# A bucket table in two parts: its first part filled uncleared from the first group on, and one register load for four row windows

## The chip, the cores and the metric

The kernel runs on one core of a Trainium2 chip. The metric is the device time of one execution in microseconds, as the median of several runs; less is better.

## The reference

Two graph layers over 6250 nodes with 128 features and 100000 edges, which are sorted by `dst`, while `src` is random:

```python
h = silu(concat([x[src], x[dst], radial(edge_weight)]) @ Wm1 + bm1)
m = silu(h @ Wm2 + bm2) @ Wm3 + bm3
out = segment_sum(m, dst)
u = silu(concat([x, out]) @ Wu1 + bu1) @ Wu2 + bu2
x = layernorm(x + silu(u @ Wi1 + bi1) @ Wi2 + bi2)

xt = logmap0(x)
att = sigmoid(concat([xt[src], xt[dst], edge_attr]) @ att_w.T + att_b)
s = xt + segment_sum(xt[src] * att, src) \
       + segment_sum(edge_attr, src) / max(count_src, 1) \
       + segment_sum(edge_attr, dst) / max(count_dst, 1)
x = layernorm(x + proj(expmap0(s)))
```

The sums over `dst` are easy, since the edges come in that order. The sums over `src` need the 100000 rows of `edge_attr` moved into an order by `src`, and this is what the change is about.

## The kernel before

**Stages.** The edges go in 98 groups (`NG`) of 1024, each as eight blocks `b` of 128 rows (one row per partition). An opening stage writes the projected node features `p_src` and `p_dst` to DRAM. The edge loop runs over the groups. The node rounds run over the 49 blocks of 128 nodes, four at a time, so 13 rounds. The attention stage runs over the groups again. A final stage sums the last rows and writes the output.

**Bucket tables.** A block of 128 nodes is a bucket, and there are 49 (`NB`). A row of `edge_attr`, with a one, the attention weight and the node's number within its bucket beside it (`RW` = 132 values), is sent to its `src` bucket by an indirect DMA on POOL (`scatter`, L814), 128 rows at a time. Blocks 0 to 2 of every group go to the table `early` (`first_t`, 896 rows for each bucket, `FIRST`). Blocks 3 to 7 go to four tables `late`, one for each stretch of groups (`GENS`: from group 0, 31, 62 and 83). The attention stage reads the tables back bucket by bucket (`bucket_load`, L1567), and TensorE sums the rows with one-hot matrices.

**Slots.** `place(g)` gives each row of group g its slot: TensorE counts how many rows went to the same bucket before (`rank`), and VectorE adds the bucket's beginning (`first`) and writes the row numbers to `to_i` (L1139). Rows that find no slot go to dump rows at the table's end (`dumps`). A group's first scatter needs `to_i` of that group.

**Clears.** Every bucket surely gets 640 of the 896 rows of `early`; the rest may stay empty and is set to zero first (`fills`, `clear`): nine DMAs for `early` (of the last bucket all rows, of the 48 others rows 640 to 895, 32 rows of each at a time), and 29 for `late`. They are issued on SP in the edge loop, two in each of the first five groups and then one in every second group (L1277). The scatters to `early` wait for the clears of `early`.

**The order of the edge loop** is written by hand. In group g, for each half, SP issues the loads `lw` of the `p_dst` rows of group g+2 (`load_rows`: four windows, for each a register load of its first row and a DMA), `near` of group g+2, `attr` of group g+1, and a clear; POOL issues four gathers (`ga`, L1080) of group g+2 and then at most one scatter to `early` of group g; TensorE, ScalarE and VectorE do the two layers of group g, and VectorE does `prepare` and `place` of group g+1:

```python
if clear and (g < LAG - 1 or i % 4 == 0):
    nc.sync.dma_start(*clear.pop(0))
gather(g + 2, range(4 * half, 4 * half + 4))
if g < NG and early(g, half) is not None:
    scatter(g, early(g, half), attrs[g][0][:, early(g, half)])
```

`early(g, half)` names the block that the loop scatters. Of the three early blocks of a group two are scattered in the loop. The third, and in every fifth group one more (`left`), is left to the middle. Of groups 0 to 5 (`LAG` = 6) all three are left to the middle.

**The middle** is a list of units of up to three such blocks (`middle`, `move_middle`, L1321 to L1340): SP loads the rows again, ScalarE copies the column of node numbers (L1335, L1338), POOL scatters them. Three units stand in each node round before TensorE's work; what is left comes after the last round. SP and POOL follow the written order here, the other engines a scheduler's. Units use four tiles in turn, so that a load waits for the scatter four units before.

**The attention stage** needs, for the logits of its first group, the statistics of all nodes: after the last round come `rstd` (L1455), norms and logarithms (L1468 to L1494), and their split into three bfloat16 parts. ScalarE then writes the attention weights into the rows of blocks 3 to 7 (L1666, L1669), and POOL scatters them to `late`.

Of the kernel before, what the change touches and what calls it, by code (L numbers as in the profile page):

```python
# [16 lines left out]
P = 128  # L17
# [9 lines left out]
ET = mybir.EngineType  # L27
# [504 lines left out]
W = 64  # L532
WE = 256

RW = 132


EARLY = ((1, 2), (0, 2), (0, 1))
LATE = (3, 4, 5, 6, 7)


LAG = 6

# [15 lines left out]
FIRST = (896, 640)  # L559
GENS = ((0, 512, 304), (31, 512, 304), (62, 384, 192), (83, 256, 116))  # L560
# [42 lines left out]
def window_path(ctx, tc, bad, x, src, dst, edge_attr, edge_weight, Wm1, bm1, Wm2, bm2, Wm3, bm3,  # L603
                Wu1, bu1, Wu2, bu2, Wi1, bi1, Wi2, bi2, att_w, att_b, out):
    nc = tc.nc
    ordered = ExitStack()
    ordered.enter_context(tc.manual_schedule())
    N, F = x.shape
# [17 lines left out]
    def windows(g):  # L626
        return min(4, NWIN - 4 * g)
# [5 lines left out]

    first_t = dram.tile([NB * FIRST[0] + 6 * P, RW], F32, name="early")
    lates = [dram.tile([NB * cap + 10 * P, RW], F32, name=f"late{j}") for j, (_, cap, _) in enumerate(GENS)]

    early_of = dram_disjoint_views(first_t[:, :], 6)
    lates_of = [dram_disjoint_views(t[:, :], 10) for t in lates]

    def stretch(g):  # L640
        return sum(g >= lo for lo, _, _ in GENS) - 1

    def table_of(g, b):

        return early_of[b + g % 2 * 3] if b < 3 else lates_of[stretch(g)][b - 3 + g % 2 * 5]

# [12 lines left out]
    dumps = const.tile([P, len(GENS), 2, 8], F32, name="dumps")  # L659
    nc.vector.memset(caps[:, :, :3], float(FIRST[0]))  # L660
    for j, (_, cap, _) in enumerate(GENS):
        nc.vector.memset(caps[:, j, 3:], float(cap))
        for b0, n, c in ((0, 3, FIRST[0]), (3, 5, cap)):
            nc.gpsimd.iota(dumps[:, j, :, b0:b0 + n], pattern=[[n * P, 2], [P, n]], base=NB * c,
                           channel_multiplier=1, allow_small_or_imprecise_dtypes=True)
# [52 lines left out]
    NL = 12  # L718
# [58 lines left out]
    first = sent.tile([P, 8, NG], F32, name="first")  # L777
    base_i = keep.tile([1, 4, NG], I32, name="base_i")
    badc = keep.tile([P, 1], F32, name="badc")
# [90 lines left out]
    with tc.tile_pool(name="init", bufs=1) as init, \  # L870
# [70 lines left out]
        def spread():  # L941
            pbase = initp.tile([P, 4, P], F32, name="pi")
            for k in range(4):
                nc.tensor.matmul(pbase[:, k, :NG], lhsT=basex[:, k], rhs=ident[:NG, :NG],
                                 start=True, stop=True)
            nc.vector.tensor_copy(base_i, pbase[:1, :, :NG])
            nc.vector.tensor_copy(baseb, pbase[:, :, :NG])
# [20 lines left out]
        def begins():  # L968

            for b0, b1, lo, hi_, cap in [(0, 3, 0, NG, FIRST[0])] + [  # L970
                    (3, 8, GENS[j][0], GENS[j + 1][0] if j + 1 < len(GENS) else NG, GENS[j][1])
                    for j in range(len(GENS))]:
                nc.vector.tensor_scalar(first[:, b0:b1, lo:hi_], hif[:, 0, b0:b1, lo:hi_], float(cap),
                                        None, op0=OP.mult)
# [77 lines left out]
    with tc.tile_pool(name="ework", bufs=2, reuse_waits="tile") as ework, \  # L1052
# [13 lines left out]

        def load_rows(g):
            for k in range(windows(g)):
                at = nc.values_load(base_i[0:1, k, g:g + 1], engines=(ET.SP,), min_val=0,
                                    max_val=ROWS - W, skip_runtime_bounds_check_because="clamped")  # L1070
                nc.sync.dma_start(lws[(4 * g + k) % NL][:W], p_dst[bass.ds(at, W)])

# [49 lines left out]
        def place(g):  # L1122
# [11 lines left out]

            over = ework.tile([P, 8], F32, name="over")
            nc.vector.tensor_tensor(over, slot, caps[:, j], op=OP.is_ge)
            nc.vector.tensor_add(slot, slot, first[:, :, g])
            nc.vector.scalar_tensor_tensor(slot, over, 1e6, slot, op0=OP.mult, op1=OP.add)
            nc.vector.tensor_tensor(to_i[:, :, g], slot, dumps[:, j, g % 2], op=OP.min)  # L1139

            for q, (end, cap, lo) in enumerate((
# [80 lines left out]
        def add_up(i):  # L1222
            g, k0, kk = part_of(i)
            if kk <= 0:
                return
            ps = sums.pop(i)
            for k in range(kk):
                at = nc.values_load(base_i[0:1, k0 + k, g:g + 1], engines=(ET.DVE,), min_val=0,
                                    max_val=ROWS - W, skip_runtime_bounds_check_because="clamped")
# [34 lines left out]
        prepare(0, 1)  # L1264
        place(0)
        for g in range(NG + 2):
            for half in range(2):
# [100 lines left out]
    with tc.tile_pool(name="nwork", bufs=2, reuse_waits="tile") as nwork, \  # L1368
# [5 lines left out]
        base_f = nwork.tile([P, NW], F32, name="bits", bufs=1)[:1]  # L1374
        nc.vector.tensor_copy(base_f, base_i.rearrange("o k g -> o (k g)"))
        pw_ = npp.tile([F, 4, P], F32, name="pu")
# [174 lines left out]
    with tc.tile_pool(name="bwork", bufs=2, reuse_waits="tile") as bwork, \  # L1551
# [4 lines left out]
        def bucket_load(us):  # L1556

            nonlocal n_load
            at = n_load % 4 * BR * RW
            n_load += 1  # L1560
            bts = []
            for i, h0, nh in us:
                t, cap = AT[i]
                c = cap // P
                bt = acc[:, 2, at:at + nh * c * RW].rearrange("p (h c f) -> p h c f", h=nh, f=RW)
                at += nh * c * RW
                nc.sync.dma_start(  # L1567
                    bt.rearrange("p h c f -> p h (c f)"),
                    t[h0 * cap:(h0 + nh) * cap].rearrange("(h p c) f -> p h (c f)", p=P, c=c))
                bts.append(bt)  # L1570
            return bts
# [278 lines left out]
```

## Time and profile before

| | |
|---|---|
| median of three runs | 2189.34 us (2189.02 to 2191.48) |
| the profiled execution: its time | 2187.51 us |
| the profiled execution: its span | 2185.6 us |
| mean granted TensorE clock | 0.85 |
| indirect DMAs on POOL | 782 gathers, 782 scatters |
| DMA moved | 412.75 MB, mean 189 GB/s |

The edge loop's gathers begin at 43.7 us of the span and its last scatter starts at 1275.6; the middle's scatters go from 1281.5 to 1446.3, the attention stage's from 1449.7 to 2090.6; the rest is the final stage. An indirect DMA's bar on POOL is the time that the engine spends on issuing it; the transfer itself lands later. "issue" as a releaser means that the engine waited for nothing that the profile shows. In a line of the timeline the first number is the start, the second the duration, and the bracket at the end holds the idle time before the instruction and what ended it. A wait for several semaphores is put down to the one that came last by the profile.

### The profile page before, as it was taken

To read this page: it belongs to the slowest core of one execution; us is meant where nothing else is said; L and a number is where in the kernel's file an instruction comes from. 1 tells how busy PE (TensorE), PEld (TensorE's weight loads), DVE (VectorE), ACT (ScalarE), POOL (GpSimd) and SP (SyncE) were. 2 spreads that over 40 slices of the span, in tenths; PEclk is the share of its full clock that TensorE was granted. 3 is DMA by queue.
4 is the path that set the end of the run, shared out by engine and by line. 5 is a ranking of instruction groups with operands and counts; after the bars stand their busy time and mean duration, and the time that the engine had idled before them with its cause. 6 is when DMAs were issued, how large, how long until landed. Compare 5 with 4: busy or idle time off the path is not lost. (4 is left out here: it accounts for less than half of the span.)

```text
span 2185.6 us, 41598 instructions
## 1 busy us (share of the span) xinstructions
PE 1674.5 (77%) x13317; PEld 1471.6 (67%) x13317; DVE 1637.3 (75%) x4255; ACT 920.9 (42%) x1580; POOL 1547.0 (71%) x1598
## 2 busy tenths in 40 slices
PE   6778798888778778788878898857777877787642
PEld 5667787777767677677767764446777767677642
DVE  7668888788778788777787854577666876867768
ACT  3755666656556565656555621222111100000016
POOL 3747777777777777777777767777777777777710
PEclk9889898999889899999999977868767987967876
DMA  7777666665666665555454545468888987988832
GB/s 211 199 186 192 173 176 170 169 167 157 177 163 157 166 173 137 137 138 139 134 138 136 137 113 158 121 210 270 255 262 282 305 276 245 314 259 284 271 120 78
DMA packets 344163, 412.75 MB, mean 189 GB/s; under 512 B 53109, under 2 KB 260347, under 8 KB 343681
## 3 DMA queue, kind: packets, MB, share of 16 engines
q1 hardware_dynamic: 292584, 303.65, 48.9%
q0 software_dynamic: 50624, 105.02, 16.4%
q8 instruction: 108, 1.77, 0.3%
q10 hardware_dynamic: 728, 1.33, 0.2%
q14 instruction: 119, 0.97, 0.1%
HBM read 319.79 MB, written 90.00 MB: 187 GB/s over the span
## 5 line engine op out<-in xcount | busy, mean ns | idle before, releaser
L1080 POOL DMA_INDIRECT ga<-p_src,src_i x782 | 751.0, 960 | 270.0 <-issue 208.2
L1596 PE MATMUL pb<-acc,oh 128*128 128x130 f32 x1960 | 326.7, 337 | 64.2 <-DVE oh L1580 34.5
L814 POOL DMA_INDIRECT late<-attr,to_i x298 | 300.8, 1009 | 94.0 <-issue 75.6
L1596 PEld LDWEIGHTS pb<-acc,oh 128*128 128x128 f32 x1960 | 306.9, 246 | 71.6 <-issue 68.2
L1214 PE MATMUL ps<-hot,h 128*128 128x64 f32 x1564 | 296.4, 272 | 0.0
L1188 ACT ACTIVATE h<-pa,bm1c 128x512 f32<-128x512 f32 x196 | 134.5, 686 | 359.2 <-PE pa L1185 358.1
L1230 DVE TENSOR_TENSOR acc<-acc,ps 128x192 f32 x391 | 137.8, 353 | 179.6 <-PE ps L1218 114.1
L1182 PE MATMUL pa<-ident,ga 128*128 128x128 f32 x782 | 162.7, 303 | 138.6 <-DMA ga<-p_src,src_i 128.6
L1199 PEld LDWEIGHTS pb<-wm,h 128*128 128x128 f32 x1564 | 233.5, 214 | 39.4 <-issue 11.9
L1214 PEld LDWEIGHTS ps<-hot,h 128*128 128x128 f32 x1564 | 243.0, 196 | 0.0
L1185 PE MATMUL pa<-feat,lw 128*128 128x256 f32 x782 | 240.6, 438 | 1.4 <-ACT feat L1110 1.4
L1199 PE MATMUL pb<-wm,h 128*128 128x128 f32 x1564 | 230.2, 295 | 1.3 <-ACT h L1188 1.3
L1182 PEld LDWEIGHTS pa<-ident,ga 128*128 128x128 f32 x782 | 100.0, 149 | 170.9 <-DMA ga<-p_src,src_i 168.1
L814 POOL DMA_INDIRECT early<-attr_row,to_i x166 | 166.9, 1005 | 67.2 <-issue 35.0
L1654 PE MATMUL pg<-a,ohT 128*128 128x49 bf16 x2346 | 104.5, 192 | 115.9 <-DVE ohT L1640 115.1
L1216 PE MATMUL ps<-hot,attr 128*128 128x64 f32 x976 | 189.9, 277 | 0.0
L1654 PEld LDWEIGHTS <-ohT 128*128 128x128 bf16 x2346 | 95.8, 101 | 133.9 <-DVE ohT L1640 133.1
L1580 DVE TENSOR_TENSOR oh<-beside,acc 128x896 f32<-128x896 f32 (+3 forms) x149 | 150.7, 1028 | 40.5 <-DMA acc<-late 37.9
L1185 PEld LDWEIGHTS pa<-feat,lw 128*128 128x128 f32 x782 | 157.5, 223 | 17.5 <-ACT feat L1110 1.8
L1640 DVE TENSOR_SCALAR ohT<-los,part 128x2048 bf16<-128x2048 bf16 x98 | 74.8, 764 | 124.6 <-DMA los<-row_lo 124.2
L1666 ACT ACTIVATE attr<-lg,attb 128x5 f32<-128x5 f32 (+1 forms) x60 | 18.2, 304 | 338.2 <-DMA late<-attr,to_i 161.3
L1201 ACT ACTIVATE h<-pb 128x512 f32<-128x512 f32 x196 | 116.4, 594 | 83.6 <-PE pb L1199 78.2
(331 smaller groups left out, 3778.1 us busy)
## 6 DMA issues: line engine op xcount, KB each, us to landing
los<-row_lo SPq DMA_DIRECT2D x98, 512.0 KB
near<-in_edge_weight_dram SPq DMA_DIRECT2D x97, 256.0 KB
attr<-in_edge_attr_dram SPq DMA_DIRECT2D x97, 256.0 KB
acc<-late SPq DMA_DIRECT2D x44, 528.0 KB
acc<-early SPq DMA_DIRECT2D x49, 462.0 KB
late<-zrow SPq DMA_DIRECT2D x22, 792.0 KB
attr<-in_edge_attr_dram SPq DMA_DIRECT2D x256, 64.0 KB
attr<-in_edge_attr_dram SPq DMA_DIRECT2D x118, 128.0 KB
```

The lines of the kernel that those rows point to most:

```text
L814: nc.gpsimd.indirect_dma_start(out=t, out_offset=bass.IndirectOffsetOnAxis(ap=to_i[:, b, g:g + 1], axis=0), in_=rows_, in_offset=None)
L1080: nc.gpsimd.indirect_dma_start(out=gas[g][:, b], out_offset=None, in_=p_src[:, :], in_offset=bass.IndirectOffsetOnAxis(ap=src_i[:, b, g:g ...
L1182: nc.tensor.matmul(pa[:, j], lhsT=gas[g][:, 2 * k0 + j], rhs=ident, is_transpose=True, start=j == 0, stop=False)
L1185: nc.tensor.matmul(pa[:, 2 * k:2 * k + 2], lhsT=lws[(4 * g + k0 + k) % NL], rhs=feats[g][:, k0 + k], start=False, stop=k == kk - 1)
L1188: nc.scalar.activation(hid1[i][:, :2 * kk], pa[:, :2 * kk], AF.Silu, bias=bm1c)
L1199: nc.tensor.matmul(pb[:, j], lhsT=h1[:, j], rhs=wm2, start=False, stop=j == nb - 1)
L1214: nc.tensor.matmul(ps[:, k, 0], lhsT=h2[:, 2 * k + c], rhs=hot[:, b], start=k == 0 and c == 0, stop=False)
L1216: nc.tensor.matmul(ps[:, k, 1], lhsT=head[:, b, :F] if b < 3 else rest[:, b - 3], rhs=hot[:, b], start=False, stop=False)
L1230: nc.vector.tensor_add(acc[:, :, bass.ds(at, W)], acc[:, :, bass.ds(at, W)], ps[:, k])
L1580: nc.vector.tensor_tensor(oh.rearrange("p h c e -> p (h c) e"), cols_p[:, None, :].to_broadcast([P, nh * c, P]), bt.rearrange("p h c f -> ...
L1596: nc.tensor.matmul(pb[:, h], lhsT=oh[:, a + h, j], rhs=bt[:, a + h, j, :S], start=j == 0 and h == 0, stop=j == c - 1 and h == n - 1)
L1654: nc.tensor.matmul(pg[:, b, :NB], lhsT=ohT[:, 0, b], rhs=a3[q], start=q == 0, stop=q == 2)
```

## The change

The table `early` gets two parts: the first holds 640 rows of each bucket (`LO`), the second, behind it, 256 more (`HI`). Groups 0 to 30 write only to the first part, with a capacity of 640. From group 31 on a row with a slot of 640 or more goes to the second part (`part2`), and the capacity is 896 as before. The first part isn't cleared, but for the last bucket, whose 640 rows are cleared by one DMA in the opening stage. The second part is cleared by nine DMAs as before, so the loop still issues 38 clears, now all at one in every second group.

With this `LAG` is gone: groups 0 to 5 scatter in the edge loop like all others. Ten scatters move there from the middle (12, less one that `left` names in each of groups 0 and 5), which shrinks from 128 to 118. ScalarE's copy of the node numbers is made for these groups too, and that of group 0 ahead of the loop.

`bucket_load` reads the table `early` by two DMAs for each bucket, of 5 and 2 rows per partition, where it was one of 7. `base_i` is stored with the four windows of a group side by side, and `load_rows` loads the four first rows by one register load of SP in place of four. `place` has three more VectorE operations for groups 31 to 97, and one check more at group 30.

```diff
-LAG = 6
 def early(g, half):
-    if g < LAG or left(g) == EARLY[g % 3][half]:
+    if left(g) == EARLY[g % 3][half]:
         return None
...
-    first_t = dram.tile([NB * FIRST[0] + 6 * P, RW], F32, name="early")
+    LO, HI = FIRST[1], FIRST[0] - FIRST[1]
+    LOW = NB * LO + 6 * P
+    first_t = dram.tile([LOW + NB * HI + 6 * P, RW], F32, name="early")
-    early_of = dram_disjoint_views(first_t[:, :], 6)
+    early_of = [dram_disjoint_views(t, 6) for t in (first_t[:LOW], first_t[:, :])]
...
-        return early_of[b + g % 2 * 3] if b < 3 else ...
+        return early_of[stretch(g) > 0][b + g % 2 * 3] if b < 3 else ...
...
+        nc.sync.dma_start(first_t[(NB - 1) * LO:NB * LO].rearrange("(p r) f -> p r f", p=P),
+                          zrow[:, None, :RW].to_broadcast([P, LO // P, RW]))
...
         def load_rows(g):
+            _, at = nc.values_load_multi_w_load_instructions(
+                base_i[0:1, g, :windows(g)], engines=(ET.SP,), min_val=0, max_val=ROWS - W, ...)
             for k in range(windows(g)):
-                at = nc.values_load(base_i[0:1, k, g:g + 1], engines=(ET.SP,), ...)
-                nc.sync.dma_start(lws[(4 * g + k) % NL][:W], p_dst[bass.ds(at, W)])
+                nc.sync.dma_start(lws[(4 * g + k) % NL][:W], p_dst[bass.ds(at[k], W)])
...
             nc.vector.tensor_tensor(over, slot, caps[:, j], op=OP.is_ge)
+            if j:
+                nc.vector.tensor_scalar(part2, hif[:, 0, :3, g], float(HI - LO), float(LOW - LO),
+                                        op0=OP.mult, op1=OP.add)
+                nc.vector.scalar_tensor_tensor(part2, slot[:, :3], float(LO), part2,
+                                               op0=OP.is_ge, op1=OP.mult)
             nc.vector.tensor_add(slot, slot, first[:, :, g])
+            if j:
+                nc.vector.tensor_add(slot[:, :3], slot[:, :3], part2)
...
-        clear = [f for t, cap, lo in [(first_t,) + FIRST] + [(t,) + g[1:] for t, g in zip(lates, GENS)]
-                 for f in fills(t, cap, lo)]
+        clear = fills(first_t[LOW:], HI, 0) + [f for t, g in zip(lates, GENS) for f in fills(t, *g[1:])]
...
         place(0)
+        nc.scalar.copy(attrs[0][0][:, :, F + 2], lof[:, :3, 0])
...
-                if clear and (g < LAG - 1 or i % 4 == 0):
+                if clear and i % 4 == 0:
                     nc.sync.dma_start(*clear.pop(0))
...
-                if LAG <= g + 1 < NG and half == 1:
+                if g + 1 < NG and half == 1:
                     nc.scalar.copy(attrs[g + 1][0][:, :, F + 2], lof[:, :3, g + 1])
...
-    middle += [[(g0 + i, b) for i, b in t] for g0 in range(0, LAG, 3)
-               for t in (((0, 1), (1, 2), (2, 0)), ((2, 1), (0, 2), (1, 0)))]
-    rest = [(g, left(g)) for g in range(LAG, NG) if left(g) is not None]
+    rest = [(g, left(g)) for g in range(NG) if left(g) is not None]
...
-                nc.sync.dma_start(
-                    bt.rearrange("p h c f -> p h (c f)"),
-                    t[h0 * cap:(h0 + nh) * cap].rearrange("(h p c) f -> p h (c f)", p=P, c=c))
+                for c0, c1, r0 in ((0, LO // P, 0), (LO // P, c, LOW)) if i == 0 else ((0, c, 0),):
+                    n = (c1 - c0) * P
+                    nc.sync.dma_start(
+                        bt[:, :, c0:c1].rearrange("p h c f -> p h (c f)"),
+                        t[r0 + h0 * n:r0 + (h0 + nh) * n].rearrange("(h p c) f -> p h (c f)", p=P, c=c1 - c0))
```

More of the change, by code (lines that the diff above doesn't have):

```diff
@@ L643, in table_of @@
     def table_of(g, b):
-        return early_of[b + g % 2 * 3] if b < 3 else lates_of[stretch(g)][b - 3 + g % 2 * 5]
+        return early_of[stretch(g) > 0][b + g % 2 * 3] if b < 3 else lates_of[stretch(g)][b - 3 + g % 2 * 5]
     row_lo = dram.tile([NG, 2, GE], BF16, name="row_lo")
@@ L659, in window_path @@
     dumps = const.tile([P, len(GENS), 2, 8], F32, name="dumps")
-    nc.vector.memset(caps[:, :, :3], float(FIRST[0]))
+    nc.vector.memset(caps[:, 0, :3], float(LO))
+    nc.vector.memset(caps[:, 1:, :3], float(FIRST[0]))
     for j, (_, cap, _) in enumerate(GENS):
         nc.vector.memset(caps[:, j, 3:], float(cap))
-        for b0, n, c in ((0, 3, FIRST[0]), (3, 5, cap)):
-            nc.gpsimd.iota(dumps[:, j, :, b0:b0 + n], pattern=[[n * P, 2], [P, n]], base=NB * c,
+        for b0, n, lo in ((0, 3, LOW + NB * HI if j else NB * LO), (3, 5, NB * cap)):
+            nc.gpsimd.iota(dumps[:, j, :, b0:b0 + n], pattern=[[n * P, 2], [P, n]], base=lo,
                            channel_multiplier=1, allow_small_or_imprecise_dtypes=True)
@@ L777, in window_path @@
     first = sent.tile([P, 8, NG], F32, name="first")
-    base_i = keep.tile([1, 4, NG], I32, name="base_i")
+    base_i = keep.tile([1, NG, 4], I32, name="base_i")
     badc = keep.tile([P, 1], F32, name="badc")
@@ L945, in spread @@
                                  start=True, stop=True)
-            nc.vector.tensor_copy(base_i, pbase[:1, :, :NG])
+            nc.vector.tensor_copy(base_i.rearrange("o g k -> o k g"), pbase[:1, :, :NG])
             nc.vector.tensor_copy(baseb, pbase[:, :, :NG])
@@ L968, in begins @@
         def begins():
-            for b0, b1, lo, hi_, cap in [(0, 3, 0, NG, FIRST[0])] + [
+            for b0, b1, lo, hi_, cap in [(0, 3, 0, NG, LO)] + [
                     (3, 8, GENS[j][0], GENS[j + 1][0] if j + 1 < len(GENS) else NG, GENS[j][1])
@@ L1067, in load_rows @@
         def load_rows(g):
+            _, at = nc.values_load_multi_w_load_instructions(
+                base_i[0:1, g, :windows(g)], engines=(ET.SP,), min_val=0, max_val=ROWS - W,
+                skip_runtime_bounds_check_because="clamped")
             for k in range(windows(g)):
-                at = nc.values_load(base_i[0:1, k, g:g + 1], engines=(ET.SP,), min_val=0,
-                                    max_val=ROWS - W, skip_runtime_bounds_check_because="clamped")
-                nc.sync.dma_start(lws[(4 * g + k) % NL][:W], p_dst[bass.ds(at, W)])
+                nc.sync.dma_start(lws[(4 * g + k) % NL][:W], p_dst[bass.ds(at[k], W)])
         def gather(g, bs):
@@ L1135, in place @@
             over = ework.tile([P, 8], F32, name="over")
+            part2 = ework.tile([P, 3], F32, name="part2")
             nc.vector.tensor_tensor(over, slot, caps[:, j], op=OP.is_ge)
+            if j:
[3 more added lines that the diff above has]
+                                               op0=OP.is_ge, op1=OP.mult)
             nc.vector.tensor_add(slot, slot, first[:, :, g])
+            if j:
+                nc.vector.tensor_add(slot[:, :3], slot[:, :3], part2)
             nc.vector.scalar_tensor_tensor(slot, over, 1e6, slot, op0=OP.mult, op1=OP.add)
             nc.vector.tensor_tensor(to_i[:, :, g], slot, dumps[:, j, g % 2], op=OP.min)
+            if g + 1 == GENS[1][0]:
+                most = ework.tile([P, 1], F32, name="most")
+                nc.vector.tensor_reduce(most, counts[:, 0], AX.X, OP.max)
+                nc.vector.tensor_scalar(most, most, float(LO), None, op0=OP.is_gt)
+                nc.vector.tensor_tensor(badc, badc, most, op=OP.max)
             for q, (end, cap, lo) in enumerate((
@@ L1227, in add_up @@
             for k in range(kk):
-                at = nc.values_load(base_i[0:1, k0 + k, g:g + 1], engines=(ET.DVE,), min_val=0,
+                at = nc.values_load(base_i[0:1, g, k0 + k:k0 + k + 1], engines=(ET.DVE,), min_val=0,
                                     max_val=ROWS - W, skip_runtime_bounds_check_because="clamped")
                 nc.vector.tensor_add(acc[:, :, bass.ds(at, W)], acc[:, :, bass.ds(at, W)], ps[:, k])
-        clear = [f for t, cap, lo in [(first_t,) + FIRST] + [(t,) + g[1:] for t, g in zip(lates, GENS)]
-                 for f in fills(t, cap, lo)]
+        clear = fills(first_t[LOW:], HI, 0) + [f for t, g in zip(lates, GENS) for f in fills(t, *g[1:])]
+        assert len(clear) < NG // 2
         turned = ework.tile([F, 2, P], F32, name="turned", bufs=1)
@@ L1374, in window_path @@
         base_f = nwork.tile([P, NW], F32, name="bits", bufs=1)[:1]
-        nc.vector.tensor_copy(base_f, base_i.rearrange("o k g -> o (k g)"))
+        nc.vector.tensor_copy(base_f.rearrange("o (k g) -> o k g", g=NG), base_i.rearrange("o g k -> o k g"))
         pw_ = npp.tile([F, 4, P], F32, name="pu")
```

## The prediction

> **What bounds the kernel now.** I read the page's busy row first, then the windows by stage, the waits of POOL, and the timelines around the places where POOL stood still.
>
> ```profile
> PE 1674.5 (77%) x13317; PEld 1471.6 (67%) x13317; DVE 1637.3 (75%) x4255; ACT 920.9 (42%) x1580; POOL 1547.0 (71%) x1598
> L1080 POOL DMA_INDIRECT ga<-p_src,src_i x782 | 751.0, 960 | 270.0 <-issue 208.2
> ```
>
> The busy row names PE, but POOL's 71% hides its issue time: 208.2 us over 683 gathers is 0.30 us ahead of each, so a gather occupies 1.25 us and a scatter (994 or 969 ns) 1.30 in the edge loop, 1.27 later. The windows by stage (start:end, length, then busy time and count of PE, PEld, DVE, ACT, POOL) show the rest:
>
> ```profile
> 44.00:158.00 114.00, 77.28 (x490) 67.34 (x489) 77.60 (x227) 65.99 (x81) 66.84 (x69) 0.83 0.78 204
> 158.00:1277.00 1119.00, 921.77 (x6500) 817.22 (x6499) 906.13 (x2516) 676.28 (x822) 850.69 (x880) 0.91 0.59 155
> 1277.00:1450.00 173.00, 130.37 (x486) 73.56 (x486) 86.57 (x274) 38.78 (x113) 125.20 (x129) 0.72 0.46 131
> 1450.00:2092.00 642.00, 485.02 (x5449) 456.18 (x5446) 460.97 (x906) 85.36 (x389) 492.14 (x488) 0.79 0.86 272
> ```
>
> In 158 to 1277, 880 instructions take 1119 us: 1.27 each, so POOL is full. In 1450 to 2092 it is full too (488 x 1.31 = 642). It is not full in the first row (69 x 1.25 = 86 of 114 us) and at two places of the third. The waits of POOL from 43 to 158 name the loss, and its timeline dates it:
>
> ```profile
> POOL early L814 <- DVE feat L1107: 17.0, 1, 17.0
> POOL ga L1080 <- DMA ga<-p_src,src_i: 11.0, 4, 4.2
> ...
> 139.84 0.95 POOL L1080 DMA_INDIRECT ga<-p_src,src_i  x1 [3.44 <-DMA ga<-p_src,src_i]
> 157.77 1.01 POOL L814 DMA_INDIRECT early<-attr_row,to_i  x1 [16.97 <-DVE feat L1107]
> ```
>
> The 17 us stand at the first scatter, that of group 6. The named L1107 is one of many semaphores; `to_i` of group 6 (L1139) was written at 151.1 and its column copied by ACT at 150.2, which leaves a clear of `early`, the last of them issued at 142.60. The gather waits fall in the same stretch, where two clears of 792 KB per group hold the DMA share at 0.88 (79 to 142 us); from 160 on, with one clear in two groups, POOL waits for nothing but issue.
>
> **Part 1: ten scatters move into groups 0 to 5.** Twelve come into the loop, less the two that `left` sends to the middle for groups 0 and 5; the middle shrinks from 128 to 118. The wait for the clears goes: the first part is never cleared but for the last bucket's 640 rows, and the second part's clears are first needed at group 31. POOL's time to the first scatter of group 6 becomes 157.77, minus the waits beyond issue (16.7 + 3.1 + 4.2 + 3.4 less 3 x 0.3 = 26.5), plus 10 x 1.30 = 13.0: 144.3, a gain of 13.5 us. All work after it in the loop is POOL's string of 1.27 us, so it moves as a whole.
>
> What is late next is `place(g)` on DVE. `to_i` was written at 70.5, 77.2, 89.7, 102.9, 117.0, 132.1 and 151.1 for groups 0 to 6. The scatters in POOL's new order would start at 76, 82.4, 95, 107.6, 120.2, 133 and 144.3: only the last is behind even at the old pace. That pace was set by loads: ACT's L1109 waited for `near` until 110.85 and 126.94, each 5 us after its issue at 106.10 and 121.81, and SP's four `lw` loads took 8.7 to 10.1 us behind two clears against 3.6 to 4.0 at 500 us. With a quarter of the clears I expect DVE's some 10.5 us per group (its busy row at 500 us). So the gain lies between 157.8 - 151.1 = 6.6 (old pace) and 13.5; I take 13.5, as the stretch 160 to 184, also with few clears, has no wait. A wait on POOL would hold the gathers queued behind it, and so PE's transposes. The six ACT copies of `lof` that come with the scatters (193 ns each) go into ACT idle time, 58% of the span; the one for group 1 stands behind a zero copy that ended at 81.8, just ahead of its scatter at 82.4.
>
> **Part 2: the middle is 10 scatters shorter, 12.7 us of POOL.** Not all of it can be kept. After its last middle scatter POOL already waited for the logits of group 0:
>
> ```profile
> 1444.82 1.44 POOL L814 DMA_INDIRECT early<-attr,to_i  x1 [0.30 <-issue]
> 1449.74 0.96 POOL L814 DMA_INDIRECT late<-attr,to_i  x1 [3.48 <-ACT att L1669]
> ...
> 1426.70 0.19 ACT L1338 COPY attr<-lof 128x1 f32<-128x1 f32 x1 [1.20 <-DMA early<-attr,to_i]
> 1428.20 0.34 ACT L1455 ACTIVATE rstd<-mv,eps 128x49 f32<-128x49 f32 x1
> 1431.93 0.19 ACT L1338 COPY attr<-lof 128x1 f32<-128x1 f32 x1 [1.26 <-DMA early<-attr,to_i]
> 1432.02 0.24 ACT L1468 ACTIVATE pn<-pn 128x49 f32<-128x49 f32 x1
> ```
>
> The node rounds keep their pace, since each round's `x` load on SP follows nine middle loads as before (last one at 1405.55, relative to the loop's end). The chain behind them (round, `rstd`, logarithms, `w3`, first logits) becomes the limit, and POOL idles from about 1433.5 (old clock). But the chain shortens: in ACT's order of the changed program no copy of a middle unit stands between the last round and `rstd` or between `rstd` and `pn`. `rstd` waited until 1428.20; DVE was through at 1424.9, so its reciprocal comes 3.6 us earlier; `pn` was ready at 1430.25 and started at 1432.02: 1.7 more. Against that, ACT's order puts one copy more ahead of round 11's second Silu (the copy ran at 1416.36, the Silu at 1414.92): 1.4 us later. Sum: 3.9, taken as 4. Bounds: 0, if that order costs what it frees, and 12.7, if POOL stays the limit.
>
> **Part 3: costs beside other work.** `place` gets three operations on 128x3 in 67 groups. The rows of its neighbours (L1137 183 ns, L1138 173) give 3 x 67 x 0.18 = 36 us of DVE time, 0.54 per group, of 12.2 us per group with 9.9 busy. `to_i` leads: its write for group 36 ends at 508.3, when POOL starts the first scatter of group 34. Cover gone, it would cost 36 us; I take 0. On the gathers beside it: their mean is 960 ns, their fastest 944, so all 2516 DVE instructions of the loop cost POOL about 0.016 x 782 = 12.5 us together, and 201 more cost 1.
>
> The Trainium skill ("SBUF — State Buffer", "SBUF: two separate sides") says that VectorE in a two-port mode locks GpSimd out for a whole instruction, so that its descriptors wait. Worked out from that, an estimate: 201 x 0.17 = 34 us lost if every new operation hit a busy POOL; the row of the gathers speaks for 1.
>
> The first table is read in two pieces: 49 further loads on SP between 1447 and 1739, at 377 ns median 18 us of issue, beside it SP's waits for landed scatters in that stretch (L1627, L1623, L1567), 122 us or 2.7 per group. The bytes are the same. I take 0; bounds 0 and 18, the issue on the path. One register load for four removes 293 loads from SP, which waits in steady state: 0. The clear of the last bucket adds one issue, about 0.4 us, before the `p_src` stores that wait for PE: 0.
>
> **Sum.** 13.5 + 4 - 1 = 16.5. Against the profiled execution (span 2185.6, its time 2187.51) 2171.0; the median of the runs is 1.8 above it, 2189.34, which gives 2172.8. I say 2173. A run tells 0.2%, 4.4 us, from no change.
>
> **Rivals.**
> - The ramp gains half: if DVE keeps its old pace, group 6's scatter waits for 151.1. For it: DVE there waits for `near` rather than for POOL. Against: the waits stand behind the clears. Gain 6.6 + 4 - 1 = 9.6: 2180. Chance 0.13.
> - The middle gives all of its 12.7 us: for it, ACT's last copies also paced the rounds; against, SP's loads did so as well. 13.5 + 12.7 - 1 = 25: 2164. Chance 0.08.
> - The change gains nothing visible: the middle's chain lengthens and the ramp stays at the old pace, 2185 to 2193. Chance 0.06.
> - Slower: SP becomes the bound of the attention stage. By the program's semaphores each SP transfer waits for the one eight before; an iteration goes from six to seven, so at POOL's 6.4 us per group transfers may take 8/7 x 6.4 = 7.3 us to land, not 8.5. Above 7.3 it decides: at 8.4 us an iteration takes 7.35, 0.95 x 49 = 47 us lost, net 2219. Against: the table piece issued at 1447.71 was in use at 1451.36, and the DMA share there is 0.86, not 1. Chance 0.06.
>
> The forecast holds 0.67, within 2168 to 2178. The range 2162 to 2182 adds the half ramp and the full middle. Faster 0.88, same 0.06, slower 0.06.
>
> **What would show it.** Right: POOL's first scatter at about 76 and no wait over 0.5 us from 44 to 160; group 6's first scatter near 144; the loop's last scatter near 1263; before the first `late` scatter an idle time of about 11 us, released by ACT; POOL at 1.27 to 1.31 per instruction after it. Wrong: scatters of groups 1 to 6 released by DVE or ACT; that idle time near zero or above 15; in the attention stage idle time of POOL released by ACT with DVE waiting for `los`; gathers whose mean rises above 975 ns.

## The result and the profile after

The changed kernel takes 2168.01 us (median of six runs, 2164.64 to 2171.29), the kernel before 2189.38 beside it. The ratio is 0.990 with a 95% interval of 0.9887 to 0.9913, so 19 to 25 us less; the forecast was 2173 in a range of 2162 to 2182. One of the five executions of the kernel with the late tables' loads split, below, took 2842.55 us where the others took 2163.84 to 2170.76; it is in no ratio, no trace of it was kept, and its cause is open. The profiled execution took 2166.28 us with a span of 2164.5, which is 21.1 us shorter than the one of before.

The busy row and the groups of the gathers and of the loop's scatters (line, engine, operation, out<-in, count, busy time, mean ns of one, idle time before them and what ended it):

```profile
PE 1676.0 (77%) x13317; PEld 1479.9 (68%) x13317; DVE 1667.4 (77%) x4460; ACT 920.6 (43%) x1576; POOL 1543.2 (71%) x1598
L1087 POOL DMA_INDIRECT ga<-p_src,src_i x782 | 750.5, 960 | 258.7 <-issue 209.4
L818 POOL DMA_INDIRECT early<-attr_row,to_i x176 | 175.9, 999 | 53.6 <-issue 40.2
```

VectorE has 30 us more work in 205 more instructions; a gather still takes 960 ns. The shares hardly move, which is why they say so little about the bound. The windows by stage do better (start:end, length, busy time and count of PE, PEld, DVE, ACT, POOL, then PE clock, DMA share, GB/s):

```profile
44.00:158.00 114.00, 84.31 (x553) 74.63 (x553) 86.51 (x255) 74.38 (x93) 87.01 (x89) 0.83 0.69 190
158.00:1260.00 1102.00, 913.43 (x6408) 816.24 (x6407) 923.64 (x2686) 666.91 (x812) 837.34 (x868) 0.90 0.61 159
1263.00:1440.00 177.00, 144.55 (x613) 86.10 (x613) 95.60 (x292) 38.84 (x111) 123.34 (x127) 0.70 0.52 150
1440.00:2070.00 630.00, 469.48 (x5307) 441.70 (x5305) 452.05 (x886) 82.72 (x378) 481.67 (x480) 0.80 0.85 268
```

In the first stretch POOL now runs 89 instructions where 69 ran, at a DMA share of 0.69 in place of 0.78: 114 / 89 = 1.28 us each, so it is full. The loop after it (1102 / 868 = 1.27) and the attention stage (630 / 480 = 1.31) are as full as before. Only the third row, the middle, has room left.

POOL's waits from 44 to 160 (engine, line, releaser: sum, times, longest), and its timeline at the first scatter, at the first scatter of group 6 and where the middle ends:

```profile
POOL ga L1087 <- issue: 20.7, 68, 0.3
...
POOL ga L1087 <- DMA ga<-p_src,src_i: 0.6, 2, 0.3
```

```profile
73.86 1.01 POOL L818 DMA_INDIRECT early<-attr_row,to_i  x1 [0.30 <-issue]
...
142.53 0.99 POOL L818 DMA_INDIRECT early<-attr_row,to_i  x1 [0.30 <-ACT feat L1117]
...
1266.11 0.97 POOL L818 DMA_INDIRECT early<-attr,to_i  x1 [6.53 <-DVE bits L1396]
...
1415.17 0.97 POOL L818 DMA_INDIRECT early<-attr_last,to_i  x1 [0.30 <-issue]
1428.53 0.97 POOL L818 DMA_INDIRECT late<-attr,to_i  x1 [12.39 <-DMA los<-row_lo]
```

No wait over 0.3 us is left in the ramp. The 17 us at the first scatter and the 10.7 at three gathers are gone, and one wait has grown, from 3.5 to 12.4 us: the one ahead of the attention stage. Its label names a load of `los`, but ScalarE's `att` (L1692) of the first group was issued only at 1428.16, and that is what the scatter sends.

Where the 21.1 us came from, by the two profiles:

| stretch | before | after | gain |
|---|---|---|---|
| start to first gather | 43.72 | 41.55 | 2.2 |
| first gather to first scatter of group 6 | 114.05 | 100.98 | 13.1 |
| from there to the end of the loop's last scatter | 1118.80 | 1117.05 | 1.75 |
| from there to the first `late` scatter | 173.17 | 168.95 | 4.2 |
| from there to the end | 735.9 | 735.9 | 0.0 |

### The profile page after: what moved, and what is told of

It is laid out like the page before. It is cut to its first block, busy times and chain, and to the rows that moved or that the text cites. A ratio compares the mean times of both kernels' runs of the same rounds, so it can differ in the third digit from the quotient of the medians.

```text
span 2164.5 us, 41635 instructions
## 1 busy us (share of the span) xinstructions
PE 1676.0 (77%) x13317; PEld 1479.9 (68%) x13317; DVE 1667.4 (77%) x4460; ACT 920.6 (43%) x1576; POOL 1543.2 (71%) x1598
## 5 line engine op out<-in xcount | busy, mean ns | idle before, releaser
L1221 PEld LDWEIGHTS pb<-wm,h 128*128 128x128 f32 x1564 | 241.8, 221 | 39.1 <-issue 13.1
L1221 PE MATMUL pb<-wm,h 128*128 128x128 f32 x1564 | 238.2, 303 | 0.7 <-ACT h L1210 0.7
L1204 PE MATMUL pa<-ident,ga 128*128 128x128 f32 x782 | 151.1, 298 | 96.1 <-DMA ga<-p_src,src_i 79.8
L818 POOL DMA_INDIRECT early<-attr_row,to_i x176 | 175.9, 999 | 53.6 <-issue 40.2
```

The costliest lines, as they stand in the source:

```text
L818: nc.gpsimd.indirect_dma_start(out=t, out_offset=bass.IndirectOffsetOnAxis(ap=to_i[:, b, g:g + 1], axis=0), in_=rows_, in_offset=None)
L1204: nc.tensor.matmul(pa[:, j], lhsT=gas[g][:, 2 * k0 + j], rhs=ident, is_transpose=True, start=j == 0, stop=False)
L1221: nc.tensor.matmul(pb[:, j], lhsT=h1[:, j], rhs=wm2, start=False, stop=j == nb - 1)
```

## Experiments

All are edits of the changed kernel, but for the last. Ratios are to the kernel before, run beside them, each from four to six runs. Their intervals are about 0.0015 to either side, so two variants that lie less than 0.002 (4 us) apart are not separated by the times; there the traces decide.

| kernel | median us | ratio | 95% interval |
|---|---|---|---|
| changed kernel | 2168.0 | 0.9900 | 0.9887 to 0.9913 |
| four register loads | 2169.5 | 0.9918 | 0.9904 to 0.9932 |
| two-part table, no scatters moved | 2169.3 | 0.9906 | 0.9891 to 0.9920 |
| two clears per group again | 2178.7 | 0.9955 | 0.9942 to 0.9968 |
| half of the scatters moved | 2165.9 | 0.9907 | 0.9888 to 0.9927 |
| late tables' loads split too | 2168.5 | 0.9907 | 0.9892 to 0.9921 |
| added operations of `place` three times | 2173.8 | 0.9917 | 0.9904 to 0.9931 |
| two middle units per round | 2172.2 | 0.9935 | 0.9920 to 0.9951 |
| and five buffers for `x` | 2162.6 | 0.9881 | 0.9866 to 0.9895 |
| two and three units in turn, five buffers | 2160.6 | 0.9865 | 0.9850 to 0.9879 |
| two units, five buffers, last copies behind the logarithms | 2161.7 | 0.9862 | 0.9843 to 0.9881 |
| and the middle's tiles in another order | 2154.0 | 0.9839 | 0.9824 to 0.9854 |

### Was it the clears or the scatters?

**No scatters moved.** Groups 0 to 5 leave all their scatters to the middle, as before; the table in two parts and the thin clears stay.

```diff
+LAG = 6
-    if left(g) == EARLY[g % 3][half]:
+    if g < LAG or left(g) == EARLY[g % 3][half]:
...
+    middle += [[(g0 + i, b) for i, b in t] for g0 in range(0, LAG, 3) for t in (...)]   # as before
```

> The changed kernel, but groups 0 to 5 scatter nothing in the loop: their ten scatters are back in the middle. The table in two parts and one clear in two groups stay. Theory (what was lost in the ramp were POOL's waits for the clears; the ten scatters only filled time that POOL gained): group 6's first scatter comes 88 to 93 us after the first gather (before 114.1, after 101.0), the middle is 12.7 us longer, and POOL's idle time ahead of the attention stage falls from 12.4 back to about 3.5. Sum against the changed kernel: -13 + 0 to 4 for place, + 12.7 - 8.9, so 2159 to 2165. Rival 1 (the ramp is paced by loads and VectorE, not by POOL): group 6's first scatter stays near 100 us after the first gather and the longer middle costs 3.8: about 2172. Rival 2 (the thinner clears bring nothing, moving the scatters does it all): near 2185.

POOL's timeline in this kernel (its scatter is on L819):

```profile
135.44 1.01 POOL L819 DMA_INDIRECT early<-attr_row,to_i  x1 [6.22 <-ACT attr_row L1324]
...
149.43 0.99 POOL L819 DMA_INDIRECT early<-attr_row,to_i  x1 [1.65 <-ACT attr_row L1324]
...
162.72 0.99 POOL L819 DMA_INDIRECT early<-attr_row,to_i  x1 [0.96 <-ACT attr_row L1324]
...
179.88 0.99 POOL L819 DMA_INDIRECT early<-attr_row,to_i  x1 [4.77 <-ACT attr_row L1324]
...
1435.21 0.97 POOL L819 DMA_INDIRECT late<-attr,to_i  x1 [3.48 <-ACT att L1694]
```

Its first gather is at 42.74, so the first scatter of group 6 comes 92.7 us after it: 21.3 earlier than before, as the theory has it. But four scatters, those of groups 6 to 9, now wait for ScalarE's copy of the node numbers, 13.6 us in sum. The copy of group 6 ended at 135.16, 1.5 us after `to_i` of that group (133.71): it stands in ScalarE's order behind the second layer's Silu of the group before, and without it `place` would be the next to wait for. So at the loop's end only 1.3 us are left of what ten scatters fewer give: from the first gather it takes 1216.8 us, 1218.0 in the changed kernel. In the middle the ten scatters stand again, and the wait ahead of the attention stage is back at 3.48; from the loop's end to the first `late` scatter it takes 175.7 us in place of 169.0. The ratio, 0.9906, is that of the changed kernel within its interval, and so the time, 2169.3, missed the expected 2159 to 2165.

So with thin clears nearly all of the gain is there without the scatters. What moving the ten scatters adds is 5.5 us by these two traces, less than the 7.3 by which two executions of the kernel before differ in the same stretch, and between -3 and +6 us by the ratios. In the loop they fill time that POOL would otherwise wait.

**Two clears per group again.** No scatter waits for a clear, but the clears are as dense as before.

```diff
-                if clear and i % 4 == 0:
+                if clear and (g < 5 or i % 4 == 0):
```

> The changed kernel with two clears in each of the first five groups again; no scatter of groups 0 to 30 waits for a clear, since they write the first part. Theory (10 of the 26.5 us of waits in the ramp were gathers and loads slowed by two clears a group): POOL's waits on gathers come back, 5 to 10 us of them between 79 and 142, and the time is 2173 to 2178. Rival (all of the loss came through the one semaphore wait of the first scatter, the gather waits were its shadow): no wait over 0.5, 2166 to 2170.

The gathers' waits came back, three of them as before:

```profile
100.78 0.94 POOL L1087 DMA_INDIRECT ga<-p_src,src_i  x1 [3.06 <-DMA ga<-p_src,src_i]
116.96 0.94 POOL L1087 DMA_INDIRECT ga<-p_src,src_i  x1 [3.85 <-DMA ga<-p_src,src_i]
132.98 0.95 POOL L1087 DMA_INDIRECT ga<-p_src,src_i  x1 [3.43 <-DMA lw<-p_dst]
```

They sum to 10.3 us (before: 3.1 + 4.2 + 3.4 = 10.7). The first scatter of group 6 came 109.8 us after the first gather, 8.8 later than in the changed kernel, and the ratio rose by 0.0055, 12 us; the median, 2178.7, is just above the expected range. Only the density of the clears differs, so they cost this much although no scatter waits for a clear. They slow SP's loads: the rows of group 6 (`attr_row`) are issued 103.6 us after the first gather, in the changed kernel after 79.0.

The 17 us at the first scatter are absent here too, but this doesn't show that they were a wait for a clear. In the kernel before, the rows that this scatter sends were late themselves:

```profile
142.60 0.33 SPq L1277 DMA_DIRECT2D early<-zrow  x1
...
153.18 0.59 SPq L857 DMA_DIRECT2D attr_row<-in_edge_attr_dram  x1
```

and in the changed kernel the same load is

```profile
120.55 1.36 SPq L861 DMA_DIRECT2D attr_row<-in_edge_attr_dram  x1
```

By the updates of their semaphore, which the two transfers of the kernel before share, its last clear of `early` had landed at 149.91, ahead of `to_i` (151.12), and the rows landed at 156.86. POOL's queue passed its wait for this semaphore at 156.88, and the scatter started at 157.77. So the 17 us ended with the rows and not with a clear: they too were the price of slow loads. In the run with dense clears the rows were issued at 145.65, 6.2 us before POOL came to the scatter. Why that is 5.9 us earlier after the first gather than in the kernel before, with clears as dense, was not tried alone. Nor was what the run keeps against the kernel before (0.0045, 10 us); the moved scatters, which fill POOL's waits, are one candidate.

**Half of the scatters moved** (`LAG = 3`: five of the ten go back to the middle).

> The changed kernel, but groups 0 to 2 scatter nothing in the loop: five of the ten scatters go back to the middle. Theory (in the ramp POOL had 6.2 + 1.7 + 1.0 us of waits for place with all ten out and none with all ten in; each scatter is free up to those waits, and costs 1.27 us beyond them): group 6's first scatter 94.5 to 97 us after the first gather, idle time ahead of the attention stage about 6: 2163 to 2167, 0 to 4 less than the changed kernel. Rival (loads and VectorE pace the ramp whatever POOL does): 101 us, and 2168 to 2171.

Group 6's first scatter came at 137.31, 95.6 us after the first gather, with one wait of 1.65 us on the way: the ramp behaves as expected. The ratio, 0.9907, is not lower than that of the changed kernel. Of what the ramp gave (5.4 us) a wait of 2.78 us at 177.95, again for ScalarE's copy, took 2.5 back, and another 2.5 went in the middle: from the loop's end to the first `late` scatter it takes 171.5 us in place of 169.0, with a wait of 7.1 at its end. The expected 0 to 4 us were at their lower end. It agrees with the run without moved scatters: with thin clears, where the ten scatters stand hardly matters.

### The edits that should cost or bring nothing

**Four register loads** in `load_rows`, from the same layout.

```diff
-            _, at = nc.values_load_multi_w_load_instructions(base_i[0:1, g, :windows(g)], engines=(ET.SP,), ...)
             for k in range(windows(g)):
+                at = nc.values_load(base_i[0:1, g, k:k + 1], engines=(ET.SP,), ...)
-                nc.sync.dma_start(lws[(4 * g + k) % NL][:W], p_dst[bass.ds(at[k], W)])
+                nc.sync.dma_start(lws[(4 * g + k) % NL][:W], p_dst[bass.ds(at, W)])
```

> The changed kernel with four register loads per group on SP in place of one; all else stays. Theory (POOL's string of indirect DMAs is the bound and SP waits in steady state): no difference beyond noise from the changed kernel's 2168, so 2164 to 2172, and group 6's first scatter still 100 to 102 us after the first gather. Rival (the earlier first gather, 41.6 against 43.7 us, and SP's shorter lw steps come from the single register load): 2171 to 2176, with the first gather again near 43.7.

The median is 1.5 us higher, the ratio 0.0018, which the intervals do not separate. The trace shows one wait of 2.3 us at the second scatter (at 81.75) and none after it in the ramp, which takes 102.3 us where 100 to 102 were expected, and the first gather at 42.05. So the register load isn't what made the opening shorter. By the trace it is worth a microsecond or two; the ratios allow 0 to 8.

**The loads of the late tables split too**: 100 more loads on SP.

```diff
+                if i:
+                    for c0, c1 in ((0, c // 2), (c // 2, c)):
+                        nc.sync.dma_start(bt[:, :, c0:c1]..., t[...][:, :, c0 * RW:c1 * RW])
```

> The changed kernel with the loads of the late tables cut in two as well: 100 more loads on SP in and after the attention stage, the same bytes. Theory (SP's issue has slack there, since it waits some 120 us for landed scatters): POOL's stretch from its first late scatter to its last grows by 0 to 3 us, 2166 to 2172. Rival (SP's eight transfers in flight or its issue decide): 100 x 0.38 = 38 us or more, with waits of POOL on ScalarE's att and of VectorE on los: 2200 to 2220.

Ratio 0.9907. POOL's waits from 1430 to 2066 begin

```profile
POOL late L818 <- issue: 116.8, 383, 0.3
POOL late L818 <- DMA late<-attr,to_i: 9.8, 32, 0.3
```

and hold none over 0.3 us. From its first `late` scatter to its last POOL took 638.3 us, 639.1 in the changed kernel. SP's waits in the stage's first 290 us, in which the 49 pieces of `early` and 15 of the 100 others are issued, were 158.9 us in the kernel before, 133.4 in the changed kernel and 133.5 here; from 1430 to 2066 they are 308 us in the changed kernel and 272 here, with 86 more loads, so SP had time to spare. The stage stays with POOL, and the slower rival, SP's eight transfers in flight, did not come even with three times the added loads.

**The added operations of `place` three times**: 402 more VectorE operations.

```diff
+            for _ in range(2 if j else 0):
+                part3 = ework.tile([P, 3], F32, name="part3")
+                nc.vector.tensor_scalar(part3, hif[:, 0, :3, g], ...)
+                nc.vector.scalar_tensor_tensor(part3, slot[:, :3], float(LO), part3, ...)
+                nc.vector.tensor_add(part3, part3, part2)
```

> The changed kernel with nine instead of three added operations of VectorE in place, for groups 31 to 97: 402 more operations of some 0.18 us, 72 us of VectorE time. Theory (place runs ahead of POOL, and the operations cost the gathers nothing that can be seen, 960 ns before and after): POOL still waits for nothing but issue in the loop, gathers' mean below 965 ns, 2166 to 2172. Rival 1 (VectorE's cover is used up: 9.9 of 12.2 us per group were busy before, 0.5 came with the change and 1.1 more here): POOL waits on to_i, 10 us or more in sum, 2178 or more. Rival 2 (operations of VectorE hold up POOL's descriptors): each costs up to its 0.18 us, gathers at 1000 ns or more, 2200 to 2240.

```profile
PE 1665.2 (77%) x13317; PEld 1476.1 (68%) x13317; DVE 1720.2 (79%) x4862; ACT 921.6 (43%) x1576; POOL 1545.0 (71%) x1598
```

VectorE is 53 us busier than in the changed kernel, POOL waits for nothing over 0.3 us from 170 to the loop's end, and a gather takes 962 ns. From first gather to the loop's end it took 1221.8 us; the changed kernel and the seven variants with the same loop and thin clears lie between 1217.4 and 1220.8. The ratio is 0.0017 higher than that of the changed kernel, not separated; the median, 2173.8, is above the theory's 2166 to 2172 and below both rivals. So 402 operations cost 1 to 4 us by the traces, and the 201 of the change half of that; the ratios alone allow 0 to 8 us. The estimate of 34 us for 201 operations, worked out from the Trainium skill ("SBUF — State Buffer", "SBUF: two separate sides"), would be 68 us here and is not seen: in this run these operations and POOL's indirect DMAs ran beside each other.

### What ended the middle

**Two units per round.** After the change the longest wait of POOL but for the opening stands ahead of the attention stage. The node rounds were given two middle units each instead of three.

```diff
-            for _ in range(3):
+            for _ in range(2):
                 move_middle()
```

> The changed kernel with two middle units in each node round in place of three; the other units come after the last round. Theory (after the change the statistics chain, not POOL, ends the middle, and the rounds are paced by SP's loads of nine rows between them): the rounds end about 30 us earlier, the idle time of 12.4 us ahead of the attention stage falls to 0 to 8 (some copies now stand ahead of rstd and the logarithms on ScalarE), 2156 to 2164. Rival (a round's own chain through TensorE, ScalarE and VectorE takes more than 7.6 us, so POOL starves between the units): waits of POOL on ScalarE's copies or the loads during the rounds add up to 10 us or more, 2168 to 2180.

The rival won: slower by 0.0035. The wait ahead of the attention stage is all but gone (2.1 us, 8 us into the stage), but POOL stood still in the rounds, for example

```profile
1325.07 0.97 POOL L818 DMA_INDIRECT early<-attr,to_i  x1 [3.81 <-DMA attr<-in_edge_attr_dram]
...
1374.21 0.96 POOL L818 DMA_INDIRECT early<-attr,to_i  x1 [4.29 <-DMA attr<-in_edge_attr_dram]
```

seven times for more than 1 us, 18.7 us in sum, for rows that were not loaded yet. SP's waits from 1262 to 1445 say why they weren't:

```profile
SPq L1423 <- DVE st L1465: 55.8, 9, 11.1
```

SP stood at the load of `x` (L1423), whose three buffers VectorE still read, and the middle's loads were queued behind it.

**Five buffers for `x`.**

```diff
-            xn = nwork.tile([P, 4, F], F32, name="xn", bufs=3)
+            xn = nwork.tile([P, 4, F], F32, name="xn", bufs=5)
```

> As the run with two middle units per node round, with five buffers for x in place of three, so that SP's x loads no longer wait for VectorE three rounds before and hold back the middle's loads behind them. Theory (the middle's end is set by the statistics chain; POOL starved in the last run only because SP stood at an x load): no wait of POOL over 1 us in the middle but the first, rounds of some 9.4 us, idle time ahead of the attention stage 0 to 5 us in place of 12.4: 2156 to 2162. Rival (the rounds are paced by the copies of the middle units in ScalarE's order, which wait for POOL's scatters anyway): idle time 8 to 13, 2164 to 2169.

SP's wait at L1423 fell from 55.8 to 10.6 us, POOL waited for nothing in the rounds, and the ratio is 0.9881 (2162.6 us, just above the theory's range). The wait ahead of the attention stage is 7.1 us, between the theory's 0 to 5 and the rival's 8 to 13. With two and three units in turn (`range(2 + b0 // 4 % 2)`) it is 7.1 as well.

> As the run above with two and three units in turn (2.5 per round, 9.5 us of POOL). Theory: rounds end some 15 us earlier than in the changed kernel, idle time 2 to 7 us, 2158 to 2164. Rival: as above, 2164 to 2169.

The time, 2160.6 (0.9865), is in the theory's range here, the wait just above it. Why 7.1 remains shows on ScalarE in the run with two units and five buffers:

```profile
1402.92 0.19 ACT L1359 COPY attr_last<-lof 128x1 f32<-128x1 f32 x1 [1.02 <-DMA early<-attr_last,to_i]
1403.12 1.28 ACT L1476 ACT_TABLE_LOAD   x1
1404.42 0.34 ACT L1476 ACTIVATE rstd<-mv,eps 128x49 f32<-128x49 f32 x1
```

`rstd` stands in ScalarE's order behind the copy for the very last middle unit. That copy waits until a scatter has freed its tile, so it came 12.7 us ahead of the last scatter (1415.58), and from the start of `rstd` to the first `late` scatter at 1423.85 it takes 19.4 us.

**The last copies behind the logarithms.** The rest of the middle's units is emitted in two parts, and the last three units' copies follow the second logarithm in ScalarE's order.

```diff
-        for _ in range(len(middle)):
+        for _ in range(len(middle) - n_middle - 3):
             move_middle()
+        with tc.manual_schedule(engines={ET.Activation}):
             nc.scalar.activation(rstd, mv[:, :, 1], AF.Sqrt, bias=eps)
...
             nc.scalar.activation(lm, y, AF.Ln, bias=1.0, scale=-1.0)
+            for _ in range(len(middle)):
+                move_middle()
```

> As the run with two units per round and five buffers for x, with ScalarE's copies of the last three middle units placed behind rstd, pn and the logarithms (an order written out for ScalarE in that stretch; POOL's and SP's order stay). Theory (of the 7.1 us that were left ahead of the attention stage the cause is ScalarE's order: rstd stood behind the last copy, which waits for a scatter 12 places ahead of the last, and from rstd to the first late scatter it takes 20.7 us): rstd comes about 9 to 11 us earlier relative to the last middle scatter, POOL waits 0 to 1 us ahead of the attention stage, 2153 to 2158. Rival (the chain needs the ScalarE copies' data or the last round itself is late): idle time 4 us or more, 2159 to 2163.

```profile
1401.88 0.34 ACT L1476 ACTIVATE rstd<-mv,eps 128x49 f32<-128x49 f32 x1 [2.06 <-DVE mv L1466]
```

```profile
1419.78 0.97 POOL L818 DMA_INDIRECT early<-attr_last,to_i  x1 [0.30 <-issue]
1422.95 0.97 POOL L818 DMA_INDIRECT late<-attr,to_i  x1 [2.20 <-ACT att L1694]
```

`rstd` is now released by VectorE's `mv` of the last round, not by a copy, and the wait is 2.2 us, 4.9 less. In this execution the loop ended 2.9 us later than in the run above, so its span (2160.5) hides that gain; the ratio, 0.9862, is below the run's above (0.9881) without being separated from it. `rstd` came 17.9 us ahead of the last middle scatter, where it stood 11 us ahead: 7 us in place of the 9 to 11 expected, since now the last round itself is late. So the time, 2161.7, is in the rival's range and not in the theory's 2153 to 2158, and the wait lies between the two.

**The middle's tiles in another order.** The middle's first unit used the tile of group 96, which TensorE reads until the end of the loop's sums; now the tile of group 95 and the extra one come first.

```diff
+    r_tiles = [r_tiles[k] for k in (2, 3, 0, 1)]
```

> As the run with the last copies behind the logarithms, and the middle's four tiles used in another order: first the one of group 95 and the extra one, which are free before the loop ends, then those of groups 96 and 97, which TensorE still reads until the loop's last sums. Theory (the 4.9 to 6.8 us between the loop's last scatter and the middle's first are the wait for group 96's tile, its load and its column copy): that gap falls below 1 us, idle time ahead of the attention stage stays 1 to 4 us (the chain's start moves with the rounds, not with the gap, so it may grow by what the gap gives), 2151 to 2157. Rival (the rounds' first x load and TensorE's last sums set the start of the rounds, and the chain behind them is the limit): the gap goes but the idle time ahead of the attention stage grows by as much, 2159 to 2163.

```profile
1259.33 0.97 POOL L818 DMA_INDIRECT early<-attr,to_i  x1 [0.30 <-issue]
1260.60 0.96 POOL L818 DMA_INDIRECT early<-attr,to_i  x1 [0.30 <-issue]
...
1280.89 0.96 POOL L818 DMA_INDIRECT early<-attr_last,to_i  x1 [2.25 <-ACT attr_last L1357]
...
1414.75 0.97 POOL L818 DMA_INDIRECT late<-attr,to_i  x1 [2.21 <-ACT att L1695]
```

The gap of 4.9 to 6.8 us between loop and middle is gone (the middle's scatters, from `attr`, follow at once), one wait of 2.25 us has come at the sixteenth of them, and the wait ahead of the attention stage stays at 2.2. The time is 2154.0 us, ratio 0.9839: below the changed kernel beyond both intervals, 14 us less than it. By the traces 13 of the 14 stand between the loop's end and the first `late` scatter: 169.0 us in the changed kernel, 164.0 with two units and five buffers, 160.2 with the last copies moved, 155.7 here. The last two steps are not separated by the ratios.

### The kernel before, once more

> The kernel before once more, for one profile. Question: the first gather was at 43.72 us of the span before and at 41.5 to 42.7 in the changed kernel and all its variants. If that is noise of the opening stage's loads, this profile shows 41.5 to 43; if the change moved it, 43.5 or more. The ramp (first gather to first scatter of group 6) should be 112 to 116 again in either case.

```profile
43.11 1.06 POOL L1080 DMA_INDIRECT ga<-p_src,src_i  x1 [22.01 <-DVE hif L958]
...
157.19 1.01 POOL L814 DMA_INDIRECT early<-attr_row,to_i  x1 [21.73 <-DMA lw<-p_dst]
```

The ramp is 114.08 us, as before to 0.03, though one of the three gather waits is missing and the wait at the first scatter is 4.8 us longer: the end of the ramp is not set by POOL's string. The rows of group 6 landed at 156.29 here, the last clear at 149.76, and POOL's queue passed that wait at 156.31. The first gather is at 43.11, between the two answers expected: two executions of before have 43.1 and 43.7, twelve, of the changed kernel and its variants, 41.55 to 42.74. The loop from group 6's first scatter to its last took 1123.9 us where the first profile had 1118.8: two executions of one kernel differ by 5 us there, which bounds what the smaller rows of the table above can tell.

## Why the prediction was right, step by step

- **What bounds the kernel.** POOL's string of indirect DMAs, held beside 77% busy time on TensorE and VectorE. The Trainium skill ("Perfetto Trace Analysis", "Identifying the Most-Contended Engine") takes the engine with the highest occupancy as the one to optimize first, and judges TensorE otherwise than by its busy time. By the busy row that would have been VectorE with 75%, ahead of POOL's 71%, while 53 us more of VectorE work lengthened the loop by 1 to 4 us, and the 13.1 us that POOL gained in the ramp were still there at the end.
- **The ramp, 13.5 us.** Measured 13.1. The sum held, but not the reading behind its largest term, and here luck had a part. The prediction left "a clear of `early`" as what ended the 17 us, since `to_i` and the column were done by 151.1; it left out the scatter's own rows, which SP issued only at 153.18 and which landed at 156.86, 7 us after the last clear. So the dependence on the clears was not what held this scatter. The term came out because the same edit makes the clears thin, and with thin clears the rows of group 6 are issued 79.0 us after the first gather in place of 109.5. That dense clears slow loads and gathers, which the prediction says of the gather waits and of `place`, is what the runs show, for both waits. The two parts of the change are unequal: the thin clears alone give 21.3 us up to the first scatter of group 6, the scatters take 8.3 of it back there, and at the loop's end the two kernels are 1.3 us apart. The doubt about `place` was well placed, but ScalarE's copy comes last: 13.6 us of waits once the scatters are out. With them in, `to_i` of group 6 was written at 132.9 and needed at 142.5.
- **The middle, 4 us.** Measured 4.2 from the loop's end to the first `late` scatter. The wait is 12.4 us, forecast 11. The terms differ: `rstd` came 3.6 us earlier as forecast (148.0 us after the loop's end in place of 151.6). From there to `pn` only 0.3 of the 1.7 came, because VectorE still had the last round's sums ahead of its reciprocal; and the 1.4 us later Silu did not cost anything. The two misses cancel.
- **Costs beside other work, 1 us lost.** The loop after the ramp was 1.75 us shorter, not 1 longer. That is less than the 5 us between two executions, so no sign can be read from it; the threefold operations put it at 0.5 to 2 us by the traces, and at 4 at most by the ratios.
- **What was not in the sum:** the opening stage, 2.2 us. This and the loop's 2.75 are why the span fell by 21.1 and not by 16.5. The step that failed, by little, is the silent one that the opening stays as it is.
- **Rivals.** The half ramp did not come, as no scatter in the ramp waits for `to_i`. The full middle did not come with this change. The SP window did not come even with 149 added loads.

The cause of the earlier first gather is open. It isn't the register load; the clear of the last bucket in the opening stage and the layout of `base_i` were not tried alone.

## What to carry to other kernels

Look for a bound in the count of instructions per window, not in the busy share: an engine with 0.30 us of issue ahead of each 0.96 us DMA is full at 76% busy. Before a wait is removed from such an engine's string, list everything that the waiting instruction needs, its own data included, with the time at which each was ready, and take the last; what is left over when two are ruled out need not be the cause. After that, ask which later wait the freed time runs into, and whether the step that now ends last stands behind work that isn't its own: here a table load and `rstd` stood behind column copies, and `x` loads ahead of row loads. Sorting those queues brought 14 us more, two thirds of what the change had brought.

## What the runs showed of the hardware that was not expected

- Clears of 792 KB, two per group, slow the gathers' and loads' landing so far that POOL waits 10 us at three gathers and SP issues the rows of group 6 24.6 us later, at a mean DMA share of 0.83 from 44 to 158 us (0.78 in the kernel before); at one in two groups (0.69) there is no wait.
- Cutting 49 table loads of 462 KB into pieces of 330 and 132 KB, and 100 further loads into halves, left the attention stage at 638 to 641 us at a DMA share of 0.85 to 0.87.
- The label of a wait changed between executions: the same 12.4 us were put down to `los` in the changed kernel and to `att` in the one with four register loads, and the wait at the first scatter of the kernel before to `feat` (17.0) and to `lw` (21.7), while in both POOL's queue passed it 0.02 us after the row load had landed.
